# One VectorE addition moved forward in a quantised GLU kernel: the next pair's first sum ahead of two additions from the third bank

## The chip, the cores and the metric

The kernel runs on one core of one Trainium2 chip. The metric is the device time of one execution in microseconds. Before the change the median of three runs is 730.92 us (730.78 to 731.84).

A core has five engines with instruction queues of their own, each of which works strictly in order: TensorE (PE in the profile; its weight loads are PEld), VectorE (DVE), ScalarE (ACT), GpSimd (POOL) and SyncE (SP, which here only issues transfers). They wait for each other through semaphores, and so does every transfer.

## The reference

The input is `x` of 4 batches x 1024 tokens x 512 features, a condition `cond` of 4 x 128, and three weights: `norm_w`, `up_w` (4096 x 512) and `down_w` (512 x 2048). What is computed, with the quantisers written out:

```python
scale = cond @ norm_w.T + 1.0
h = x * (scale[:, None, :] * rsqrt(mean(x * x, -1) + 1e-6))
val, gate = split(h @ up_w.T, 2, axis=-1)            # 2048 features each
h = val * gelu(gate)                                  # exact gelu
s = 127.0 / clip(max(abs(h), -1), 1e-5)               # one scale for each token
hq = clip(round(h * s), -128, 127) / s
t = 1.0 / clip(mean(abs(down_w)), 1e-5)
wq = clip(round(down_w * t), -1, 1) / t               # -1, 0 or 1, times a constant
y = hq @ wq.T + x
```

So each token's hidden values become whole numbers up to 127, and the down weights become -1, 0 and 1; the down product is exact in whole numbers.

## The kernel before

**Batches and slots.** A batch is 1024 tokens in two halves of 512 (`h` = 0, 1). The up-projection of a batch is cut into 16 slots (`j` = 0 to 15); slot `j` makes 128 value features and 128 gate features for the whole batch. Batch 0 is done by plain matrix products. Batches 1 to 3 use a scheme of Winograd's kind: a block product of 2 x 2 by 2 x 2 is made with seven products in place of eight, and sums of blocks stand for the eighth. Function `slot` writes out the order of a slot: products 0, 4 and 1 of this slot, product 3 of the slot before, product 5 of this slot, product 2 of the slot before, product 6 of this slot, with the activations and additions between (all matrix products of `product` have line L580; the banks are called A, B and E).

**Down pairs.** While batch `b` is in its up slots 10 to 13 (`DOWN`), for `b` = 1 and 2, the down product of batch `b`-1 is made there: one pair (class `Pair`) in each of those four slots, number `a` = 0 to 3. A pair handles 128 tokens of each half, with the same kind of scheme: its operands are blocks of quantised values (`part(h, u)`, half of tokens and half of hidden features) and sums of them. `sum1` (L827) is `part(1,0) + part(1,1)`, 128 x 1024 in bf16, and is put into a piece of the big buffer H that the next slot will fill only later. `sums` (L834 to L836) makes the other three from it. A pair has three PSUM banks, k1, k2 and k3. Its methods, in order:

- `first`: eight matrix products of `sum1`'s result into one half of k3, then eight of `part(0,0)` into its other half (L848); ScalarE copies that half into k1 (L858).
- `third`: products into k1; ScalarE copies half of k1 to k2 (L866); then two additions on VectorE take k3's first half, times a factor for each token, onto the rows of `x` in `xr`, one for each half of tokens (`onto`, L889, 128 x 256 each).
- `fourth`: products into k1 and k2, a copy on ScalarE (L875), and an addition of 128 x 512 from k1 (L889).
- `fifth`: products into k2 and an addition of 128 x 512 from k2 (L889); then the two rows go out (L884).

The rows `xr` are loaded by SP at the head of the slot (L792, `down_load`).

**What sets the order.** The order is written out by hand: the program's order of calls is each engine's order (`manual_schedule`), and semaphores are placed by the data. `slot` calls three hooks `mid[0]`, `mid[1]`, `mid[2]`: after product 5, after product 2 with its addition (L688, `E + t2`), and after product 6 with its addition (L694, `A + v`). In a slot with a pair, `early` calls `first` and `sums` before the up products of the slot, so the first matrix product of a slot reads what `sum1` wrote in the slot before. Between the slot's own work, two lists of smaller steps (`Filler`) put the maxima and the quantising on VectorE and ScalarE by written-out costs.

**The next batch's tokens.** In the same slots the next batch is prepared (`Tokens`): load (L506), squares on ScalarE (L514), scaling on ScalarE (L526) and on GpSimd (L527, two instructions of 128 x 512), sums on GpSimd (L535 to L538), splitting (L559, L563) and a transposing transfer (L566). Some of that lies in pieces of H: token group 0's split values are in the H pieces of slots 12 and 13, and are read by the transposing transfer that is queued at the end of slot 10. `sum1` for the pair of slot 12, made in slot 11, writes the H piece of slot 12, and so waits for that transfer.

Of the kernel before, what the change touches and what calls it, by code (L numbers as in the profile page):

```python
# [50 lines left out]
def glu_quant_kernel(  # L51
# [68 lines left out]
    def t_view(b):  # L120
        v = R[:, b % 2].bitcast(F16)[:, : NA * C_ALL * 2 * HALF]
        return v.rearrange("p (a c l k t) -> p a c l k t", a=NA, c=C_ALL, l=2, k=2)
# [16 lines left out]
    def s_tile(g):  # L139


        if g >= NJ:
            return SXY[:, (g + 1) % 2]
        return S_more if g % 3 == 2 else SXY[:, g % 3]

    def h_slots(g, n=1):
        s = g % NSLOT
        return H[:, s : s + n]
# [10 lines left out]
    def po_bank(name, shape=None):  # L159
        return bank("po", 3, shape, name)  # L160
# [250 lines left out]
    def s_load_x(g):  # L411
        s_load(g, Y_TO, C_ALL)
        s_load(g, 0, Y_FROM, g % NJ >= ROWS)

    def s_load_y(g):
        if g % NJ < ROWS:
            s_load(g, Y_FROM, Y_TO)
        else:
            s_load(g, Y_FROM + 1, Y_TO)
            s_load(g, Y_FROM, Y_FROM + 1, True)  # L420
# [50 lines left out]
    def w_block(name):  # L471
        k, y = W_AT[name]
        return wd8[:, :, k, :, :, y]
# [3 lines left out]
    def d_sums(ns):  # L477
        for n, c in [(n, c) for n in ns for c in range(2)]:
            o, m, l = (w_block(name) for name in D_SUMS[n])
            DVE.tensor_tensor(o[:, c], m[:, c], l[:, c], ALU.subtract, saturate=False)  # L480
# [240 lines left out]
    def get_ready():  # L721

        POOL.partition_all_reduce(ready, ready, P, bass_isa.ReduceOp.max)
# [22 lines left out]
    def token_turn(b, am, h0=0, h1=2):  # L746

        c = slice(h0 * TOK, h1 * TOK)
        SP.dma_start(out=am_dram[b : b + 1, c], in_=am[0:1, c])

    def token_undo(b, dq, h0=0, h1=2):

        n = slice(h0 * NA, h1 * NA)
        v = am_dram[b : b + 1, h0 * TOK : h1 * TOK].rearrange("o (n p) -> p (o n)", p=P)
        SP.dma_start(out=dq[:, n], in_=v)

        def bring():
            DVE.reciprocal(dq[:, n], dq[:, n])
            DVE.tensor_scalar(dq[:, n], dq[:, n], wmean, None, ALU.mult)

        return bring
# [28 lines left out]
    def down_load(b, h, a):  # L790
        xr = wpool.tile([P, D], F32, name=f"xr_{b}_{h}_{a}", tag="xr")
        SP.dma_start(out=xr, in_=xf[rows_of(b, h, a), :])  # L792
        return xr
# [410 lines left out]
    class Filler:  # L1204
# [8 lines left out]
        def run(self, now, budget):  # L1213

            n = 0
            while n < len(self.items):
                slot, cost, f, due = self.items[n]
                assert due is None or now <= due, (now, due)
                if slot > now or (cost > budget and due != now):
                    n += 1  # L1220
                    if slot <= now:
                        break
                    continue
                del self.items[n]
                budget -= cost
                f(now)
            return budget
# [33 lines left out]
    def old_places(a):  # L1261

        if a == 0:
            v = wpool.tile([P, 2, D], F32, name="sq_0", tag="xn", bufs=1)
            u = wpool.tile([P, 4, HALF], F32, name="sr_0", tag="xt", bufs=1)
            return v[:, 0], v[:, 1], u.rearrange("p n d -> p (n d)")[:, :D]
        if a == 1:
            v = wpool.tile([P, C_ALL, 2, HALF], F16, name="sq_1", tag="nx", bufs=1)
            v = v.rearrange("p c l d -> p (c l d)").bitcast(F32)
            return [v[:, n * D : (n + 1) * D] for n in range(3)]  # L1270
        v = h_slots(B * NJ, 2).rearrange("p s h t -> p (s h) t")
        return [v[:, n] for n in range(3)]

    state = {}
    for b in range(1, B):
# [3 lines left out]
        dq = state[b - 1] = sm.tile([P, 2 * NA], F32, name=f"dq_{b}", tag="dq")  # L1279
# [41 lines left out]
        for j in range(NJ):  # L1321
            g = b * NJ + j
            down = b + 1 < B and j in DOWN
            if down:
                pair, a = pairs[j], DOWN[j]
                xrs = [down_load(b - 1, h, a) for h in range(2)]
            early_sums, late_sums = D_SUM_AT.get((b, j), ((), ()))
            left = SLOT_US + PAIR_US * down - OWN_US + 0.4
            more = D_SUM_US * len(late_sums) + 0.7 * (j + 1 == min(DOWN) and b + 1 < B)
            left -= D_SUM_US * len(early_sums) + more  # L1330
            mine = {p: [sum(c[e] for _, c in steps.get((j, p), ())) for e in range(2)] for p in "xyz"}
            left -= sum(mine[p][0] for p in "xyz")
            act_left = {"x": 2.7, "y": 2.2 if down else 1.1, "z": 0}

            def run(p):
                nonlocal left
                for f, _ in steps.get((j, p), ()):
                    f()
                if p == "x":
                    cap = min(left, 3.9 - mine["x"][0] - (0 if down else mine["y"][0] + more))  # L1340
                    left -= cap - dve.run((j, p), cap)
                elif p == "z":
                    left = dve.run((j, p), left)
                if p != "z":
                    act.run((j, p), act_left[p] - mine[p][1])

            def early():
                if down:
                    pair.first([po_bank(f"po_{b}_{a}_{n}") for n in range(3)])
                    pair.sums(None, h_slots(g)[:, 0, 1])  # L1350
                d_sums(early_sums)

            def next_pair():
                if b + 1 < B and j + 1 in DOWN:
                    pairs[j + 1] = Pair(b - 1, DOWN[j + 1])
                    pairs[j + 1].sum1(h_slots(g + 1)[:, 0, 0])

            def more_sums():
                next_pair()
                d_sums(late_sums)  # L1360

            mid = [nothing] * 3
            if j + 1 == min(DOWN):
                mid[0] = more_sums
            if down:
                mid = [lambda: (pair.third(xrs, dq), d_sums(late_sums)), lambda: (pair.fourth(), next_pair()), lambda: (loads(), pair.fifth())]

            def loads():
                if NJ + 2 <= g + 2 < B * NJ:
                    s_load_x(g + 2)  # L1370
                if NJ + 2 <= g + 1 < B * NJ:
                    s_load_y(g + 1)


            def late():
                if b == 1 and j + 1 == min(DOWN):

                    banks = [po_bank(f"po_set_{n}") for n in range(3)]
                    for bank in banks[:2]:
                        PE.matmul(  # L1380
                            bank.rearrange("p (a t) -> p a t", t=P),
                            s_tile(g + 1)[:, 0, 0, :P], t_view(b)[:, :, 0, 0, 0, :],
                            start=True, stop=True,
                        )

            if b + 1 == B and j in DOWN and DOWN[j] < 3:
                pairs[DOWN[j]] = Pair(b - 1, DOWN[j])
                places = old_places(DOWN[j])
                pairs[DOWN[j]].sum1(places[0])
                pairs[DOWN[j]].sums(*places[1:])  # L1390
            if j == 4:
                token_turn(b - 1, am)
            if j == 5:
                bring_dq = token_undo(b - 1, dq)
            if j == 6:
                bring_dq()
            if j == NJ - 1:
                get_ready()
            elif b == 1 and j == 0:
                get_ready()  # L1400
            slot(g, lambda: run("x"), lambda: run("y"), lambda: run("z"), early, mid, late)
            if not down:
                loads()
# [5 lines left out]
    dq = sm.tile([P, 2 * NA], F32, name="dq_end", tag="dq")  # L1409
# [22 lines left out]
    def old_first(a):  # L1432
        old[a].first(old_banks(a))
# [27 lines left out]
    mid = (nothing, lambda: old_first(2), nothing)  # L1461
# [105 lines left out]
```

## Time and profile before

| quantity | value |
|---|---|
| median of three runs | 730.92 us (730.78, 730.92, 731.84) |
| the profiled execution: its own time | 731.92 us |
| the profiled execution: span of the trace | 730.1 us |
| TensorE busy, of the span | 719.6 us (99%) |
| VectorE busy | 580.9 us (80%) |
| ScalarE busy | 398.5 us (55%) |
| GpSimd busy | 195.9 us (27%) |
| granted TensorE clock | 1.00 |
| slots 10, 11, 12 of batch 1, from first matrix product to first matrix product | 15.17, 16.12, 15.19 us |
| the same of batch 2 | 15.18, 16.11, 15.19 us |

The profiled execution took 731.92 us by its own clock, 1.8 us more than the span from first to last instruction, and 1.00 us more than the median. In the lists of instructions by time, a row gives the start, the length, the engine, the line of the kernel and the operation with its tiles; a bracket at the end gives the idle time of the engine just before and what ended it. A row with "x8" is eight instructions in a row. The length of a group of matrix products overlaps the next group's start, since they are pipelined: eight products of 128 x 256 take 0.87 us from start to the next group's start, though the row says 1.04. "PE po L848 <- DVE H L827: 1.5, 2, 0.8" means that L848 on TensorE waited for L827 on VectorE, 1.5 us in total, 2 times, 0.8 us at most.

### The profile page before, as it was taken

How to read it: one execution, taken by the hardware profiler on the slowest of the kernel's cores; microseconds unless marked ns; L12 is line 12 of the kernel's file. 1: busy time of each engine (PE TensorE's matmuls, PEld its weight loads, DVE VectorE, ACT ScalarE, POOL GpSimd, SP SyncE). 2: the span in 40 equal slices, each digit the busy share in tenths (PEclk: the TensorE clock that was granted, in tenths of full speed). 3: DMA queues.
4: the chain of work that ended last, by engine and by line, in shares of the span. 5: the costliest groups of instructions: out<-in, count | busy, mean ns of one | idle time of the engine just before them, and what ended most of it. 6: DMA issues, size and time to landing. Idle time of an engine off the chain costs nothing.

```text
span 730.1 us, 10143 instructions
## 1 busy us (share of the span) xinstructions
PE 719.6 (99%) x3662; PEld 359.0 (49%) x3662; DVE 580.9 (80%) x819; ACT 398.5 (55%) x629; POOL 195.9 (27%) x207
## 2 busy tenths in 40 slices
PE   7999999999999999999999999999999999999998
PEld 3544444444444446555444445656444444445844
DVE  6877879886698899787689887687678888755897
ACT  5868875872336674544335676543433665333274
POOL 1379887776100033440010030361020000000100
PEclk9999999999999999999999999999999999999999
DMA  6759999998344654876735646855934555442253
GB/s 228 259 154 312 284 275 259 236 218 230 116 102 101 131 141 131 200 165 166 185 101 103 130 101 173 199 145 156 233 92 101 94 113 102 102 102 93 93 183 115
DMA packets 203982, 117.30 MB, mean 161 GB/s; under 512 B 165382, under 2 KB 174487, under 8 KB 203932
## 3 DMA queue, kind: packets, MB, share of 16 engines
q1 hardware_dynamic: 203642, 116.33, 62.7%
q8 instruction: 28, 0.46, 0.3%
q10 hardware_dynamic: 290, 0.33, 0.1%
q14 instruction: 22, 0.18, 0.1%
HBM read 54.22 MB, written 23.09 MB: 106 GB/s over the span
## 4 chain that ended last, share of the span: by engine, by line
PE 85%; DVE 6%; POOL 3%; DMA 3%; ACT 1%; issue 1%; SPq 1%; POOLq 0%; DVEq 0%; ACTq 0%
PE A L580 33%; PE E L580 17%; PE po L848 8%; PE B L580 8%; PE pg L595 6%; PE pv L595 6%; PE po_end L800 4%; DVE gm L714 1%; DMA s_dram<-R 1%; PE po L800 1%; DMA H<-in_x_dram 1%; POOL H L372 1%; DMA SXY<-H 1%; DVE R L716 1%; ACT H L313 1%
## 5 line engine op out<-in xcount | busy, mean ns | idle before, releaser
L580 PEld LDWEIGHTS <-SXY 128*128 128x128 f16 x2016 | 197.3, 98 | 232.3 <-issue 0.6
L580 PE MATMUL A<-R,SXY 128*128 128x512 f16 x1152 | 266.3, 379 | 0.0
L580 PE MATMUL E<-R,SXY 128*128 128x512 f16 x576 | 140.0, 379 | 0.1
L678 DVE SCALAR_TENSOR_TENSOR H<-A,sg,t 128x512 f32<-128x512 f32 x48 | 36.0, 750 | 69.1 <-PE A L580 69.0
L772 DVE TENSOR_TENSOR H<-H,am 128x1024 f32<-128x1024 f32 x64 | 76.2, 1216 | 0.0
L730 POOL PARTITION_ALL_REDUCE am<-R x8 | 14.4, 1794 | 229.7 <-DVE R L716 229.7
L595 PEld LDWEIGHTS <-SXY 128*128 128x128 f16 x486 | 47.5, 98 | 57.8 <-DMA SXY<-H 0.8
L691 ACT ACTIVATE t<-t,sg 128x512 f32<-128x512 f32 x48 | 34.6, 721 | 66.7 <-DVE t L688 66.5
L580 PE MATMUL B<-R,SXY 128*128 128x512 f16 x288 | 70.0, 379 | 0.0
L714 DVE TENSOR_REDUCE gm<-H 128x512 f32<-128x1024 f32 x56 | 69.0, 1233 | 1.0
L595 PE MATMUL pg<-R,SXY 128*128 128x512 f16 x252 | 57.8, 379 | 0.3 <-DMA SXY<-H 0.3
L595 PE MATMUL pv<-R,SXY 128*128 128x512 f16 x234 | 54.4, 379 | 0.2 <-DVE H L623 0.2
L675 ACT ACTIVATE t<-B,sg 128x512 f32<-128x512 f32 x48 | 33.0, 687 | 36.5 <-PE B L580 36.5
L484 POOL TENSOR_SCALAR ssq<-ssq 128x2 f32<-128x2 f32 x12 | 4.1, 340 | 173.0 <-ACT xt L514 122.2
L658 ACT COPY t<-A 128x512 f32<-128x512 f32 x48 | 28.0, 583 | 39.5 <-PE A L580 39.2
L848 PE MATMUL po<-wd,R 128*128 128x256 fp8e4 x384 | 48.5, 273 | 0.0
L780 ACT ACTIVATE H<-H 128x1024 f32<-128x1024 f32 x38 | 39.9, 1050 | 14.1 <-DVE H L772 14.0
L670 ACT COPY v<-E 128x512 f32<-128x512 f32 x48 | 28.1, 586 | 31.2 <-PE E L580 27.7
L848 PEld LDWEIGHTS <-R 128*128 128x128 bf16 (+1 forms) x416 | 40.7, 98 | 8.5
L697 DVE SCALAR_TENSOR_TENSOR H<-v,sg,t 128x512 f32<-128x512 f32 x48 | 36.8, 768 | 7.9 <-ACT t L691 7.9
L716 DVE TENSOR_TENSOR R<-R,gm 128x512 f32<-128x512 f32 x56 | 40.9, 730 | 1.3
L784 ACT ACTIVATE R<-H 128x1024 bf16<-128x1024 f32 x38 | 40.1, 1055 | 0.8
(208 smaller groups left out, 976.4 us busy)
## 6 DMA issues: line engine op xcount, KB each, us to landing
SXY<-s_dram SPq DMA_DIRECT2D x57, 256.0 KB, 3.1
s_dram<-SXY SPq DMA_DIRECT2D x18, 384.0 KB, 3.1
H<-in_L_cond_up_w_dram SPq DMA_DIRECT2D x13, 512.0 KB, 5.1
SXY<-s_dram SPq DMA_DIRECT2D x39, 128.0 KB, 3.1
xr<-in_x_dram SPq DMA_DIRECT2D x19, 256.0 KB, 3.0
out_dram<-xr SPq DMA_DIRECT2D x19, 256.0 KB, 2.5
H<-in_x_dram SPq DMA_DIRECT2D x8, 512.0 KB, 8.4
R<-in_L_cond_down_w_dram SPq DMA_DIRECT2D x8, 512.0 KB, 6.4
```

The source lines that it names most:

```text
L580: PE.matmul(o, s[:, w, k, :], tv[:, :, c, l, k, :], start=start and n == 0, stop=stop and n == len(TERMS) - 1, skip_group_check=True,)
L595: PE.matmul(ps, a[k // 2][:, w, k % 2, :], XP[:, l, k, h * TOK : (h + 1) * TOK], start=n == 0, stop=n == len(terms) - 1,)
L678: DVE.scalar_tensor_tensor(h_half(g - 1, 0), prev["A"], gain(g - 1, 0), prev["t1"], ALU.mult, ALU.mult)
L691: ACT.activation(prev["t2"], prev["t2"], AF.Gelu, scale=gain(g - 1, 1))
L697: DVE.scalar_tensor_tensor(h_half(g - 1, 1), prev["v"], gain(g - 1, 0), prev["t2"], ALU.mult, ALU.mult)
L714: DVE.tensor_reduce(gm[0], v, AX.X, ALU.max, apply_absolute_value=True)
L716: return [largest, lambda: DVE.tensor_tensor(m, m, gm[0], ALU.max)]
L772: DVE.tensor_tensor(v, v, r.to_broadcast([P, 2, TOK]), ALU.mult)
L780: ACT.activation(v, v, AF.Copy, bias=MAGIC)
L784: ACT.activation(q, by_tile(v), AF.Copy, bias=-MAGIC)
L800: PE.matmul(po.rearrange("p (y c o) -> p y c o", c=2, o=P), q[:, a, h, j], wd8[:, :, j // n, j % n, :, y0:y1].rearrange("p c o y -> p y c o"),
L848: PE.matmul(po, w[:, j], m, start=start and j == 0, stop=stop and j == n - 1, skip_group_check=True,)
```

## The change

In a slot with a pair, the making of the next slot's `sum1` (inside `next_pair`) stood in `mid[1]`, behind `fourth`. It now stands in `mid[0]`, ahead of `third`. On VectorE the order of the instructions of a slot was: the two additions from k3 (L889), `E + t2` (L688), the addition from k1 (L889), `sum1` (L827), `A + v` (L694). It is now: `sum1` (L827), the two additions from k3, L688, the addition from k1, L694.

```diff
             if down:
-                mid = [lambda: (pair.third(xrs, dq), d_sums(late_sums)), lambda: (pair.fourth(), next_pair()), lambda: (loads(), pair.fifth())]
+                mid = [
+                    lambda: (next_pair(), pair.third(xrs, dq), d_sums(late_sums)),
+                    pair.fourth,
+                    lambda: (loads(), pair.fifth()),
+                ]
```

This touches slots 10, 11 and 12 of batches 1 and 2, six instructions in all. The pair of slot 10 gets its `sum1` in slot 9 from `more_sums`, and slot 13 has no next pair; both are as before, as is batch 3. The order on TensorE, ScalarE, GpSimd and SP is the same, and so is every operand's size. The wait of slot 11's `sum1` for the transposing transfer goes with it to its new place.

## The prediction

> **What bounds the kernel now.** I read the busy times first, then TensorE's waits, then the instructions by time around the two waits that concern the change, engine by engine.
>
> The page's first part:
>
> ```profile
> PE 719.6 (99%) x3662; PEld 359.0 (49%) x3662; DVE 580.9 (80%) x819; ACT 398.5 (55%) x629; POOL 195.9 (27%) x207
> ```
>
> TensorE has work for all but about 10 us of a 730.1 us span, at a granted clock of 1.00. So a VectorE instruction matters only where TensorE waits for it. The list of TensorE's waits from 100 us to the end has two lines:
>
> ```profile
> PE po L848 <- DVE H L827: 1.5, 2, 0.8
> PE pv L595 <- DVE H L623: 0.2, 1, 0.2
> ```
>
> The first is the moved instruction: L827 is `sum1`, L848 a pair's matrix products. It holds TensorE twice. TensorE's instructions by time show where (the last group of slot 11 and the first of slot 12 in batch 1, then the latter in batch 2):
>
> ```profile
> 305.12 1.04 PE L848 MATMUL po<-wd,R 128*128 128x256 fp8e4 x8
> 306.93 1.05 PE L848 MATMUL po<-wd,H 128*128 128x256 fp8e4 x8 [0.78 <-DVE H L827]
> ...
> 477.57 1.05 PE L848 MATMUL po<-wd,H 128*128 128x256 fp8e4 x8 [0.77 <-DVE H L827]
> ```
>
> Seen here is a distance of 1.81 us from the group at 305.12 to the next one, where groups of this form follow each other after 0.87 us elsewhere (321.25 to 322.12). Without the wait the group would start at 305.12 + 0.87 = 305.99 us, and in batch 2 (the group before starts at 475.76) at 476.63. The true loss is 0.94 us each, a little over the bracket's 0.78, since the bracket counts from the modelled end of the last product. The slots' lengths agree: slot 11 takes 16.12 and 16.11 us, its neighbours 15.17 to 15.19.
>
> VectorE in slot 11, batch 1 and then batch 2:
>
> ```profile
> 300.60 1.24 DVE L714 TENSOR_REDUCE gm<-H 128x512 f32<-128x1024 f32 x1
> 302.79 0.48 DVE L889 SCALAR_TENSOR_TENSOR xr<-po,dq,xr 128x256 f32<-128x256 f32 x1 [0.96 <-DMA xr<-in_x_dram]
> 304.17 0.49 DVE L889 SCALAR_TENSOR_TENSOR xr<-po,dq,xr 128x256 f32<-128x256 f32 x1 [0.89 <-DMA xr<-in_x_dram]
> ...
> 305.82 1.05 DVE L827 TENSOR_TENSOR H<-R 128x1024 bf16<-128x1024 bf16 x1
> ...
> 474.38 0.48 DVE L889 SCALAR_TENSOR_TENSOR xr<-po,dq,xr 128x256 f32<-128x256 f32 x1 [0.20 <-DMA xr<-in_x_dram]
> ...
> 476.03 1.48 DVE L827 TENSOR_TENSOR H<-R 128x1024 bf16<-128x1024 bf16 x1
> ```
>
> VectorE stands idle in front of the two additions from k3, because the rows of `x` have not landed (L792 is issued at 299.85, behind a long transposing transfer on SP), and `sum1`, which needs nothing of those rows, is queued behind them. GpSimd adds to it:
>
> ```profile
> 303.82 2.51 POOL L527 TENSOR_TENSOR xn<-xn,sc 128x512 f32<-128x512 f32 x2 [4.14 <-ACT xn L526]
> ...
> 474.47 2.50 POOL L527 TENSOR_TENSOR xn<-xn,sc 128x512 f32<-128x512 f32 x2 [4.14 <-ACT xn L526]
> ```
>
> GpSimd's two instructions end at 306.33 and 476.97, and `sum1` ends at 306.87 and 477.51: 0.54 us later both times, however early it began (305.82, 476.03). The four other `sum1` that the change moves also end 0.54 us behind a pair of L527 (289.39 and 289.93, 321.02 and 321.56, 460.02 and 460.56, 491.32 and 491.87), while the one at 272.38, with GpSimd idle, takes 0.68. So beside L527 this instruction ends when L527 lets it. GpSimd is released by ScalarE, which follows TensorE, so both batches lose the same, though the rows of `x` landed differently.
>
> The transfer that slot 11's `sum1` must wait for, and its time from issue to landing in that stretch (batch 1, batch 2):
>
> ```profile
> 294.83 4.93 SPq L566 DMA_TRANSPOSE R<-H  x1
> ...
> 466.00 4.63 SPq L566 DMA_TRANSPOSE R<-H  x1
> ```
>
> ```profile
> R<-H SPq DMA_TRANSPOSE x1, 6.7
> ...
> R<-H SPq DMA_TRANSPOSE x1, 6.5
> ```
>
> It lands at 294.83 + 6.7 = 301.5 and at 466.00 + 6.5 = 472.5 us.
>
> **The change, slot 11.** In batch 1 VectorE is free for the moved `sum1` from 300.60 + 1.24 = 301.84 us, 0.3 us after the transfer landed. GpSimd does nothing from 299.68 to 303.82, so I take 0.68 us from the undisturbed row: it ends at 302.52, before the first addition can start (302.79). With the slowest row, 1.48 us, it ends at 303.3; the second addition waits till 304.17 all the same. In batch 2 its last instruction before (L714, 471.24) ends at 472.47 and the transfer lands at 472.5; `sum1` ends between 473.2 and 474.0, TensorE wants it at 476.63. In both, `sum1` is done at least 2.6 us before TensorE asks. So the wait goes, if nothing stands close behind it. Next in line is the bank: the same matrix products write k3, which the second addition from k3 lets go at 304.17 + 0.49 = 304.66 and at 474.86, 1.33 and 1.77 us before the products' new starts. Their weights and the other operand were ready a slot before. So each slot 11 loses its whole excess: 16.12 - 15.18 = 0.94 and 16.11 - 15.18 = 0.93 us. Ends for this term: nothing at all, if something unseen stands at the same place, and 1.87, since TensorE loses no more there.
>
> **The change, slots 10 and 12.** Here `sum1` was in time already (done 0.88 and 0.56 us ahead of TensorE in batch 1, 0.90 and 0.89 in batch 2), so nothing is to be gained, and the question is what now comes later: the two additions from k3 (which free k3 for the next slot's first product), L688 (which ScalarE's gelu L691 waits for), and the addition from k1. `A + v` (L694) and all that follows has the same work in front of it as before.
>
> Batch 2 hides it simply. VectorE has 0.73 us idle in front of L688 in both slots, and the new starts (456.15, and 487.45 less the shift) lie more than a microsecond before L527 (457.52, 488.82), so `sum1` takes 0.68 and L688 starts within 0.1 us of its old time: cost 0.
>
> In batch 1, slot 10, `sum1` would start at 286.78, beside L527 (286.88 to 289.39). If it comes first it takes 0.68; if it waits for both instructions of L527 it ends at 289.93, the two additions take 0.87 more, and k3 is free at 290.7, with TensorE asking at 290.81. Slot 12 is the densest stretch: `sum1` would start near 318, and L527 sits there, 0.94 us earlier than before, from 317.3 to 320.1. At worst `sum1` ends at 320.1 + 0.54 = 320.6, k3 is free at 321.5, and TensorE asks at 322.12 - 0.94 = 321.18: a cost of 0.3 us. If it gets in after the first instruction of L527 (half of 2.83 us: 318.7), k3 is free at 320.1 and the cost is 0. I take 0, which all but the full hold give, and keep +0.3 as the end. L691 may start up to 1.1 us later in slot 12; what it feeds, L697, writes values that are not read on TensorE's way before the next batch, so this costs nothing. If L527 is held by `sum1` instead, its sums (done at 293.06 in slot 10) are read by L559 at 301.25: 8 us of cover.
>
> The Trainium skill's page "SBUF — State Buffer", section "SBUF: two separate sides", says that VectorE and GpSimd share a pair of ports as an exclusive lock, held for a whole instruction, also by a VectorE instruction with two SBUF inputs against a GpSimd one that reads SBUF. That fits the six ends 0.54 us behind L527, and it speaks against the change in slots 10 and 12, where `sum1` now meets L527 at its start. By the page the lock is given up between the two instructions, which would put that cost at 0 and the sum at -1.87; by the worst reading of the rows the sum is -1.57.
>
> **Queues.** SP, GpSimd, ScalarE and TensorE keep their orders. SP's L884 behind `fifth` waits for an addition that in slot 11 comes no later than before (L694 moves from 306.80 to about 305.8, the addition after it waits for TensorE until 306.2). The wait for the transfer is now in front of two additions, L688 and the addition from k1; but the rows of `x` are issued on SP behind that same transfer, so those additions could not start before it anyway.
>
> **The sum.** -0.94 - 0.93 + 0 = -1.87 us. TensorE has no other wait from slot 12 to the end, and the steps that feed it there (loads of weights, transposed tokens, scales) are released by TensorE or by VectorE's work, which moves forward with it. The last transposing transfer of batch 2's tokens is the closest I found: issued at 346.30, landing some 6.4 us later at 352.7, first read near 355.4, so 2.7 us of cover against a shift of 0.94. The profiled execution's own 731.92 us would become 730.05; it stands 1.00 us above the median, so the median of 730.92 becomes 729.05, or 0.26% less.
>
> **The rivals.** (1) The wait changes its owner: TensorE waits for k3 instead, as rows of `x` that land later would hold the additions. For it: the rows land late (304.17, 474.38). Against it stand 1.33 and 1.77 us of room. With half of one place's gain and the worst of slot 12, it comes to 730.92 - 1.87 + 0.47 + 0.3 = 729.8. The case that the timed executions lose less there than the profiled one belongs here too.
>
> (2) Slower: slot 11's `sum1` is held by the transposing transfer, with the additions behind it. It lands at 301.5 and 472.5; from landing on, `sum1` and two additions need 0.68 + 0.87 us, so TensorE waits only for a landing after 304.4 and 475.1, and the kernel gets slower than before only from 305.4 and 476.0 on, 3.5 us late. The twelve transfers of this line landed 6.0 to 7.5 us after issue, so about 1 us of scatter is seen. At 4.5 us late in both the price is 2 x 1.0 us: 732.9.
>
> (3) The change does nothing: TensorE waits in truth for something else at 306.93. Against it: the weight load of the same products, which reads only `sum1`'s result, starts at 306.93 as well, 0.06 us after `sum1` ends, and in batch 2 also. Time: 730.9.
>
> **How the numbers follow.** About 0.2% (1.46 us) is what a measurement of this kernel can tell from no change, and the predicted gain is only 0.41 us beyond it, with runs that spread over 1.06 us. The forecast has 0.72, of which I give 0.05 to scatter that hides it; rival 1 has 0.18, of which 0.03 still reaches 0.2%; rival 3 has 0.06, rival 2 0.04. Faster: 0.72 - 0.05 + 0.03 = 0.70. Slower: 0.04. Same: the rest, 0.26. The range goes from 728.4 (the whole gain and 0.65 us of scatter, somewhat over half of the runs' spread) to 730.5 (rival 1 and 0.7 us of scatter); rivals 2 and 3 are left out.
>
> **What would show it.** Right: TensorE's list of waits has no L827, the slots 11 take 15.2 us, `sum1` of slot 11 starts at about 301.8 and 471.6 (the second 0.94 earlier than now reckoned) and takes near 0.7, and the additions start still at the rows' landing. The step for slots 10 and 12 is wrong if a slot after them starts late with TensorE waiting for L889. The prediction as a whole is wrong if a new wait of about 0.9 us stands at slot 12's start with another releaser, or if TensorE's shift of 0.94 is lost again before slot 0 of the next batch.

## The result and the profile after

The changed kernel takes 730.02 us (median of 22 runs, 728.83 to 731.95), the kernel before, timed beside it, 731.61 us (median of 22 runs, 729.67 to 734.85). The ratio is 0.9978, with a 95% interval of 0.9968 to 0.9988: 0.22% faster, 1.6 us between the medians. The runs spread with the granted clock: the fifteen of the changed kernel with a mean of 0.999 or 1.000 have a median of 729.62 us, the seven with 0.997 or 0.998 one of 731.39. The profiled execution took 730.04 us, with a span of 728.3 us against 730.1 before.

The list of TensorE's waits from 100 us to the end has lost its first line:

```profile
PE pv L595 <- DVE H L623: 0.2, 1, 0.2
```

TensorE's instructions by time, the last group of slot 11 and the first of slot 12, in batch 1 and in batch 2:

```profile
305.14 1.04 PE L848 MATMUL po<-wd,R 128*128 128x256 fp8e4 x8
306.01 1.04 PE L848 MATMUL po<-wd,H 128*128 128x256 fp8e4 x8
...
474.83 1.04 PE L848 MATMUL po<-wd,R 128*128 128x256 fp8e4 x8
475.71 1.04 PE L848 MATMUL po<-wd,H 128*128 128x256 fp8e4 x8
```

The groups now follow each other after 0.87 and 0.88 us, where 1.81 us lay between them before. VectorE in slot 11 of batch 1 (start, length, instruction, idle time in front of it):

```profile
300.62 1.24 DVE L714 TENSOR_REDUCE gm<-H 128x512 f32<-128x1024 f32 x1
301.77 0.69 DVE L827 TENSOR_TENSOR H<-R 128x1024 bf16<-128x1024 bf16 x1
302.67 0.48 DVE L889 SCALAR_TENSOR_TENSOR xr<-po,dq,xr 128x256 f32<-128x256 f32 x1 [0.22 <-issue]
303.74 0.48 DVE L889 SCALAR_TENSOR_TENSOR xr<-po,dq,xr 128x256 f32<-128x256 f32 x1 [0.58 <-DMA xr<-in_x_dram]
```

`sum1` fills time in which VectorE stood idle. The second addition still starts when its row lands; for the first the bracket names no releaser ("issue"), so that it waits for its row is not shown here. All six slots with a moved `sum1` take 15.18 us from first product to first product; slot 11 took 16.12 and 16.11. By batch 2's slot 13 TensorE is 1.88 us ahead of before (a group of the pair's products there stands at 502.15 against 504.03), and it keeps that to the end: 730.1 - 728.3 = 1.8 us.

One more place is worth a look, for what follows. In slot 12 of batch 1, `sum1` took 1.76 us. VectorE's instructions and GpSimd's L527 there, before the change and then after it:

```profile
317.97 0.68 DVE L716 TENSOR_TENSOR R<-R,gm 128x512 f32<-128x512 f32 x1
...
320.61 0.95 DVE L827 TENSOR_TENSOR H<-R 128x1024 bf16<-128x1024 bf16 x1
...
318.19 2.83 POOL L527 TENSOR_TENSOR H<-H,sc 128x512 f32<-128x512 f32 x2 [2.03 <-ACT H L526]
```

```profile
316.87 0.68 DVE L716 TENSOR_TENSOR R<-R,gm 128x512 f32<-128x512 f32 x1
317.47 1.76 DVE L827 TENSOR_TENSOR H<-R 128x1024 bf16<-128x1024 bf16 x1
319.15 0.86 DVE L889 SCALAR_TENSOR_TENSOR xr<-po,dq,xr 128x256 f32<-128x256 f32 x2
...
317.25 3.11 POOL L527 TENSOR_TENSOR H<-H,sc 128x512 f32<-128x512 f32 x2 [2.19 <-ACT H L526]
```

After the change the two additions let k3 go at 320.01 and TensorE asks at 321.19, so nothing waits in this execution.

### The profile page after: what moved, and what is told of

Its sections match the earlier page's. It is cut to its first block, busy times and chain, and to the rows that moved or that the text cites. A ratio compares the mean times of both kernels' runs of the same rounds, so it can differ in the third digit from the quotient of the medians.

```text
span 728.3 us, 10143 instructions
## 1 busy us (share of the span) xinstructions
PE 719.1 (99%) x3662; PEld 359.2 (49%) x3662; DVE 578.8 (79%) x819; ACT 398.7 (55%) x629; POOL 194.9 (27%) x207
## 4 chain that ended last, share of the span: by engine, by line
PE 84%; DVE 5%; POOL 3%; DMA 3%; ACT 2%; issue 1%; SPq 1%; POOLq 0%; ACTq 0%; DVEq 0%
PE A L580 33%; PE E L580 17%; PE po L848 8%; PE B L580 8%; PE pg L595 6%; PE pv L595 5%; PE po_end L800 4%; DVE gm L714 1%; PE po L800 1%; DMA H<-in_x_dram 1%; ACT H L313 1%; POOL R L387 1%; DMA SXY<-H 1%; DMA xa<-in_x_dram 1%; DVE R L716 1%
## 5 line engine op out<-in xcount | busy, mean ns | idle before, releaser
L595 PEld LDWEIGHTS <-SXY 128*128 128x128 f16 x486 | 47.5, 98 | 57.9 <-DMA SXY<-H 0.8
L595 PE MATMUL pg<-R,SXY 128*128 128x512 f16 x252 | 57.8, 379 | 0.3 <-DMA SXY<-H 0.3
L595 PE MATMUL pv<-R,SXY 128*128 128x512 f16 x234 | 54.4, 379 | 0.2 <-DVE H L623 0.2
L697 DVE SCALAR_TENSOR_TENSOR H<-v,sg,t 128x512 f32<-128x512 f32 x48 | 37.6, 783 | 7.9 <-ACT t L691 7.9
L694 DVE TENSOR_TENSOR v<-A,v 128x512 f32<-128x512 f32 x48 | 32.8, 684 | 11.8 <-PE A L580 10.6
L716 DVE TENSOR_TENSOR R<-R,gm 128x512 f32<-128x512 f32 x56 | 40.9, 731 | 1.3
```

Source lines behind the costliest of these rows:

```text
L595: PE.matmul(ps, a[k // 2][:, w, k % 2, :], XP[:, l, k, h * TOK : (h + 1) * TOK], start=n == 0, stop=n == len(terms) - 1,)
L697: DVE.scalar_tensor_tensor(h_half(g - 1, 1), prev["v"], gain(g - 1, 0), prev["t2"], ALU.mult, ALU.mult)
L716: return [largest, lambda: DVE.tensor_tensor(m, m, gm[0], ALU.max)]
```

## The experiments

The theory to test: the gain is slot 11's wait alone. The wait before was made of two things, rows of `x` that landed late in front of `sum1`, and GpSimd's L527, which held `sum1` when it came to run. The rivals: slots 10 and 12 have a share; the rows alone, or GpSimd alone, made the wait; the transfer that `sum1` waits for can turn the gain into a loss. In all of them the lengths of slots are taken from first product to first product, and "excess" is what a slot has over 15.18 us. The ratio beside two medians is an estimate of its own, with its 95% interval in brackets; it can differ from the quotient of the medians by 0.1%.

**Slot 11 alone (e1)**

```diff
+front = j == 11
-    lambda: (next_pair(), pair.third(xrs, dq), d_sums(late_sums)),
-    pair.fourth,
+    lambda: (next_pair() if front else None, pair.third(xrs, dq), d_sums(late_sums)),
+    lambda: (pair.fourth(), None if front else next_pair()),
```

> Only slot 11's first sum stands in front; slots 10 and 12 keep the order of before. Theory (all of the gain is slot 11's wait): TensorE has no wait for the first sum in the down slots, slot 11 takes 15.18 us in batches 1 and 2, and the time is 1.87 us below the kernel before, a ratio of 0.9974, the same as the full change. Rival (the order in slots 10 and 12 does something too, for better or worse): the time differs from the full change's by more than 0.3 us, and slots 10 to 12 differ from it in the trace.

Measured: 730.14 us against 731.46, ratio 0.9976 (0.9965 to 0.9987), as for the full change. Slot 11 has no excess in either batch. But the profile has a new wait, in a slot that was quiet before. TensorE, VectorE and GpSimd of that execution around slot 12 of batch 1:

```profile
321.99 1.05 PE L848 MATMUL po<-wd,H 128*128 128x256 fp8e4 x8 [1.19 <-DVE H L827]
...
317.00 1.76 DVE L716 TENSOR_TENSOR R<-R,gm 128x512 f32<-128x512 f32 x1
...
320.73 1.21 DVE L827 TENSOR_TENSOR H<-R 128x1024 bf16<-128x1024 bf16 x1
...
316.69 3.20 POOL L527 TENSOR_TENSOR H<-H,sc 128x512 f32<-128x512 f32 x2 [1.78 <-ACT H L526]
```

Slot 12 takes 16.53 us. L527 began 0.3 us ahead of L716 here, L716 took 1.76 us in place of 0.68, and `sum1`, at its old place behind it, came too late for a TensorE that asks 0.94 us sooner. So slot 12 isn't idle ground. The timed runs do not show this loss as clearly as the profile, whose own time (730.87 us) is the slowest of its eight.

**Slots 10 and 12 alone (e2)**, the condition of e1 turned round (`j != 11`).

> Only the first sums of slots 10 and 12 stand in front; slot 11 keeps the order of before. Theory: nothing is gained or lost, ratio 1.000; slot 11 still takes 16.1 us and TensorE still waits 0.8 us twice for the first sum; in slot 12 of batch 1 the first sum is held by GpSimd's scaling and takes 1 us or more, with TensorE not waiting. Rival (slots 10 and 12 share the gain or cost something): the ratio lies at 0.999 or lower, or a slot 11 or 13 starts late.

Measured: 731.74 against 731.46, ratio 0.9998 (0.9986 to 1.001): no change that can be told from none. Slot 11 of batch 1 has its excess of 0.94. In batch 2 it has none, which was not expected. There `sum1` started at 476.45, while L527 ran from 475.46 to 478.42, and it took 0.84 us: it got in before GpSimd's second instruction. In the kernel before it started at 476.03 with L527 from 474.47, inside the second one. So the old wait depends on where in L527 `sum1` falls, and a slot 11 in the old order does not lose its 0.94 us in every execution.

**Behind the two additions from k3 (e3)**

```diff
-    lambda: (next_pair(), pair.third(xrs, dq), d_sums(late_sums)),
+    lambda: (pair.third(xrs, dq), next_pair(), d_sums(late_sums)),
```

> In all three slots the first sum stands behind the two additions from k3 and in front of E + t2: later than in the change, earlier than before, and still behind the late rows of x. It starts near 304.2 to 304.6 us in slot 11 of batch 1, inside GpSimd's first scaling instruction (303.8 to 305.1). Theory (the port is given up between GpSimd's two instructions, and the first sum ends 0.54 us behind the one that it met): it ends at 305.6, 0.4 us before TensorE asks at 306.0, so the whole 1.87 us is won, with the rows as late as before: it was not needed to pass the late rows, only to begin before GpSimd's second instruction. Rival A (the late rows are the cause): some of the wait is left, 0.3 us or more in each slot 11. Rival B (GpSimd's pair holds it as one): it ends at 306.9 as before and the time is that of before.

Measured: 730.21 against 731.46, ratio 0.9981 (0.9971 to 0.9992). VectorE, GpSimd and TensorE in slot 11 of batch 1:

```profile
304.47 0.48 DVE L889 SCALAR_TENSOR_TENSOR xr<-po,dq,xr 128x256 f32<-128x256 f32 x1 [0.49 <-DMA xr<-in_x_dram]
304.87 1.06 DVE L827 TENSOR_TENSOR H<-R 128x1024 bf16<-128x1024 bf16 x1
...
304.11 2.95 POOL L527 TENSOR_TENSOR xn<-xn,sc 128x512 f32<-128x512 f32 x2 [4.14 <-ACT xn L526]
...
306.28 1.04 PE L848 MATMUL po<-wd,H 128*128 128x256 fp8e4 x8
```

`sum1` ends at 305.93, in the middle of the pair of L527, and the pair takes 2.95 us in place of 2.50: VectorE came between the two instructions. TensorE does not wait in slot 11 of either batch. Both rivals fall in this run: the rows were as late as ever, and the pair did not hold as one. This agrees with what the page "SBUF — State Buffer" of the Trainium skill says in its section "SBUF: two separate sides": whichever of the two instructions starts first holds the shared pair of ports "for the whole instruction". Slot 12 of batch 1 has an excess of 0.32 here, with L527 (317.52) ahead of L716 (318.29).

**The order of before, with the rows of `x` early and the transfer late (e4)**; **the changed order with the same (e5)**

```diff
 plan, token group 0:
-    ((6, "z"), (7, "x"), (7, "y"), (9, "y"), (10, "x"), (10, "z"))
+    ((6, "z"), (7, "x"), (7, "y"), (9, "y"), (10, "x"), (11, "x"))
```

> The order of before on VectorE, but token group 0's transposing transfer is queued on SP behind slot 11's rows of x in place of ahead of them, so the rows come early (near 300 us) and the transfer lands late, by an estimate at 304.9 us (rows issued at 297.1, transfer 1.1 later, 6.7 to land). VectorE reaches the first sum by about 304.2 and waits for the transfer. Theory (late rows plus GpSimd's second scaling instruction made the wait): if the transfer lands before 305.1 the first sum ends at 305.6 and TensorE does not wait, 1.87 us faster than before; if it lands later, the first sum ends at 306.9 and nothing is gained. Rival (only VectorE's order counts): the wait of 0.94 us stays in both batches whatever lands when.

> The changed order on VectorE, with the transposing transfer behind the rows of x: this makes the slower rival happen. The first sum now waits in front of the two additions until the transfer lands, near 304.9 us by the same estimate. Theory: it ends at 305.6, the two additions end at 306.4, and TensorE waits 0.4 to 0.5 us in each slot 11, for k3 (L889), not for the first sum: about 1 us slower than the change, 0.9 us faster than before. If the transfer lands after 305.1, the first sum ends at 306.9, the additions at 307.7, TensorE waits 1.7 us each time, and the kernel is 1.5 us slower than before. Rival (the wait for the transfer is harmless at either place): as fast as the change.

Measured for e4: 732.21 against 731.66, ratio 0.9998 (0.9983 to 1.0014). In its profile slot 11 has no excess in either batch: `sum1` waited for the transfer until 304.33, met L527 (303.70) in its first instruction and ended at 305.52, and TensorE asked at 305.87. So VectorE's order is not the only way to take this wait away, and the rival falls. Yet slot 12 of batch 1 took 16.30 us, 1.12 of excess, again with L527 (317.11) ahead of L716 (317.17). That leaves 0.75 us of gain in the profile. The 1.87 us of the theory did not come in the timed runs: six of the twelve had a mean granted clock of 0.995 to 0.998 (median 732.87 us), and the six with 0.999 or 1.000 have a median of 730.74, against 731.16 for twenty such runs of the kernel before. What each of them lost in slot 12 is not shown.

Measured for e5: 731.59 against 731.66, ratio 0.9997 (0.9985 to 1.0009). VectorE, GpSimd and TensorE of batch 1:

```profile
302.79 1.69 DVE L827 TENSOR_TENSOR H<-R 128x1024 bf16<-128x1024 bf16 x1 [2.12 <-DMA R<-H]
304.40 0.86 DVE L889 SCALAR_TENSOR_TENSOR xr<-po,dq,xr 128x256 f32<-128x256 f32 x2
...
317.07 1.76 DVE L716 TENSOR_TENSOR R<-R,gm 128x512 f32<-128x512 f32 x1
...
302.65 2.95 POOL L527 TENSOR_TENSOR xn<-xn,sc 128x512 f32<-128x512 f32 x2 [4.14 <-ACT xn L526]
...
316.56 3.40 POOL L527 TENSOR_TENSOR H<-H,sc 128x512 f32<-128x512 f32 x2 [1.58 <-ACT H L526]
...
305.32 1.05 PE L848 MATMUL po<-wd,H 128*128 128x256 fp8e4 x8 [0.33 <-DVE xr L889]
321.36 1.05 PE L848 MATMUL po<-wd,H 128*128 128x256 fp8e4 x8 [0.69 <-DVE xr L889]
```

The first wait is the slower rival: `sum1` stands still for the transfer, the additions stand behind it, and TensorE waits for k3. It costs 0.49 and 0.48 us in the two slots 11, as expected, though the transfer landed earlier than estimated (`sum1` was let go at 302.8, in an execution that reached slot 11 about 1.2 us sooner). L527 has a part in it: `sum1` met its first instruction and took 1.69 us; with 0.68 us k3 would have been free near 304.3, by an estimate, ahead of TensorE, which asked at 304.83. The second wait, 0.86 us of excess in slot 12 of batch 1, was not expected, and makes the sum 1.83 us, about what the kernel before loses. It has the same root: from `sum1` at 302.79 to L716 at 317.07 VectorE has no gap of more than 0.1 us, so what slot 11 lost in time brought L716 behind L527. So the gain hangs on where the transfer is queued.

**The order of before, with GpSimd's scaling later (e6)**

```diff
 plan, token group 2:
-    ((10, "y"), (11, "x"), (11, "y"), (13, "x"), (13, "y"), (13, "z"))
+    ((10, "y"), (11, "x"), (11, "z"), (13, "x"), (13, "y"), (13, "z"))
```

> The order of before on VectorE, but the scaling of token group 2 (ScalarE's L526 and with it GpSimd's L527) stands one place later in slot 11, behind ScalarE's gelu of that slot, so GpSimd is idle while the first sum runs. Theory (the wait was made of lateness behind the rows of x, and of GpSimd's hold on top): the first sum starts where it did (305.8 and 476.0) and takes 0.68 us, ends at 306.5 and 476.7, and TensorE's excess per slot 11 falls from 0.94 to about 0.57 in batch 1 and 0.14 in batch 2; 1.2 us faster than before. Rival A (the late rows alone): the wait stays 0.94. Rival B (GpSimd alone): the wait is gone, 1.87 us faster.

Measured: 732.14 against 731.66, ratio 1.0002 (0.999 to 1.0014); the 1.2 us of the theory did not come. Slot 11 is as expected in kind: `sum1` takes 0.68 us in both batches, and the excess falls to 0.51 and 0.40 us (0.57 and 0.14 expected; in batch 2 the second row was there 2.0 us before TensorE asked, 2.25 in the first profile of before). With GpSimd away about half of the wait stays; with the rows early and GpSimd in place (e4) none stayed. So both causes are real. But L527 and its sums now lie in VectorE's way at the head of slot 12 (L716 at 308.38 takes 1.75 us), whose excess in batch 1 is 1.98 us, and more than the gain is lost there.

**Slots 11 and 12 (e7), and second profiles (e8, e9, e10)**

The profiles of e1 and e3 to e6 all show trouble in slot 12 of batch 1, which the kernel before does not have. The theory was reworked: TensorE's 0.94 us bring L527 forward, since it follows TensorE (in all 14 profiles L527 of slot 12 in batch 1 starts 11.24 to 11.26 us after the slot's first product), and L716 on VectorE comes only just ahead of it or just behind. e7 is e1 with `front = j > 10`; e8, e9 and e10 are e1, the kernel before and the changed kernel once more.

> First sums of slots 11 and 12 in front, slot 10's where it was before. Theory, reworked after the runs so far (slot 11's move wins the wait; slot 12's move is needed in batch 1 to keep the gain, since TensorE then asks 0.94 us sooner; slot 10's move is worth nothing): TensorE has no wait in the down slots and the ratio is that of the full change, 0.9975 to 0.998. Rival (slot 10 matters too): TensorE waits at slot 11's start, or slot 10 is longer than 15.2 us.

> A second profile of the kernel with slot 11 alone moved. Theory (where VectorE's L716 meets GpSimd's L527 in slot 12 of batch 1 is settled anew in each execution): if L716 starts before L527 it takes 0.68 us and TensorE's wait at slot 13 is 0 to 0.4 us; if after, it takes 1.76 and the wait is again 1.2. Rival (the wait at slot 13 is there in every execution): 1.2 us whichever comes first.

> A second profile of the kernel before. Theory: TensorE waits for the first sum in slot 11 where the first sum starts after GpSimd's second L527 instruction, 0.8 us by the bracket, and does not where it starts earlier, as in batch 2 of the run with slots 10 and 12 alone; so one, two or no waits. Rival (the wait is the same in each execution): two waits of 0.8 us.

> A second profile of the changed kernel. Theory: no wait of TensorE for L827 or L889 from 100 us on, slots 10 to 12 at 15.2 us in both batches, first sum of slot 12 of batch 1 between 0.7 and 1.8 us. Rival (the first profile was a lucky one): a wait of 0.3 us or more in one of the slots.

e7: 730.48 against 732.2, ratio 0.9981 (0.9965 to 0.9998); slot 10 takes 15.18 us in both batches, so its `sum1` is worth nothing. The theory's other half fails: slot 12 of batch 1 has 0.66 us of excess, waiting for L889, with L527 (316.99) ahead of L716 (317.30).

e8: no wait at all, with L716 ahead of L527:

```profile
318.88 0.69 DVE L716 TENSOR_TENSOR R<-R,gm 128x512 f32<-128x512 f32 x1
...
321.53 0.95 DVE L827 TENSOR_TENSOR H<-R 128x1024 bf16<-128x1024 bf16 x1
...
319.26 2.67 POOL L527 TENSOR_TENSOR H<-H,sc 128x512 f32<-128x512 f32 x2 [2.19 <-ACT H L526]
```

So e1's wait is there in one execution and not in another, and goes with that order. (e8's own time, 732.04 us, is still longer than e1's 730.87: its slot 10 of batch 1 began at 277.67 us in place of 275.10, ahead of all that is at issue here; its granted clock in the first 50 us was 0.97, in e1 1.00.)

e9: the two old waits of 0.77 and 0.78 us, as in the first profile of the kernel before; `sum1` started in L527's second instruction both times.

e10: the changed kernel has a wait after all. TensorE, VectorE and GpSimd:

```profile
321.84 1.05 PE L848 MATMUL po<-wd,H 128*128 128x256 fp8e4 x8 [0.48 <-DVE xr L889]
...
304.25 0.48 DVE L889 SCALAR_TENSOR_TENSOR xr<-po,dq,xr 128x256 f32<-128x256 f32 x1 [0.69 <-DMA xr<-in_x_dram]
...
307.16 1.23 DVE L697 SCALAR_TENSOR_TENSOR H<-v,sg,t 128x512 f32<-128x512 f32 x1
...
307.12 0.72 POOL L536 TENSOR_TENSOR xt<-xn 128x256 f32<-128x256 f32 x1
...
317.56 1.76 DVE L716 TENSOR_TENSOR R<-R,gm 128x512 f32<-128x512 f32 x1
319.24 1.75 DVE L827 TENSOR_TENSOR H<-R 128x1024 bf16<-128x1024 bf16 x1
320.92 0.86 DVE L889 SCALAR_TENSOR_TENSOR xr<-po,dq,xr 128x256 f32<-128x256 f32 x2
...
317.25 3.19 POOL L527 TENSOR_TENSOR H<-H,sc 128x512 f32<-128x512 f32 x2 [1.78 <-ACT H L526]
```

L527 starts at the same 317.25 as in the first profile of the changed kernel, but L716 at 317.56 in place of 316.87. Now L716 waits for L527's first instruction and `sum1` for its second, and the additions behind them let k3 go at 321.78; slot 12 takes 15.83 us. Where L716 lost its 0.69 us can be read back to slot 11. There the second row of `x` let its addition go at 304.25 in place of 303.74, so L697 (value times gelu, VectorE's last work for that slot) began at 307.16 in place of 306.93. GpSimd's sum L536 begins at 307.12 in both profiles, so L697 is ahead of it in the first and behind it here, and takes 1.23 us in place of 0.77; from there to L716 VectorE has no gap of more than 0.1 us. In e12, the third profile of the change, and in e8, L697 is ahead of L536 as well; in e1 and e7 it is behind. So the order in slot 12 is settled a slot earlier, and the late rows of slot 11 have a part in it. The rival of a lucky first profile is half right.

**Slot 12's sum further forward (e11), and the change timed beside it (e12)**

```diff
-    lambda: (next_pair(), pair.third(xrs, dq), d_sums(late_sums)),
+    lambda: (next_pair() if j < 12 else None, pair.third(xrs, dq), d_sums(late_sums)),
...
-slot(g, lambda: run("x"), ...)
+slot(g, lambda: (next_pair() if down and j == 12 else None, run("x")), ...)
```

> The change, and slot 12's first sum moved further forward, ahead of the splitting of token group 1 (L563) and of L716, near 314.8 us, about 2 us before GpSimd's L527 of that slot. Theory (what the change still loses is slot 12 of batch 1, where L527 may come ahead of L716 and then of the first sum): the first sum takes 0.7 us, L716 may still take 1.76, the additions from k3 end near 320.2, 1 us before TensorE asks at 321.2; no wait in any slot, whichever comes first, and a time 0.3 us below the change on average. Rival (the later work in slot 12 eats it): a wait for L889 of 0.3 us or more at slot 13's start remains.

> The changed kernel once more, timed beside the version with slot 12's first sum further forward. Theory: ratio to before 0.9975 to 0.9985; in the profile either no wait, if L716 starts before L527 in slot 12 of batch 1, or a wait of TensorE of about 0.5 us for L889 at slot 13's start, if after. Rival: a wait that does not go with that order.

Measured: e11 730.08 against 731.42, ratio 0.9976 (0.9966 to 0.9986); e12 729.8, ratio 0.9981 (0.997 to 0.9992). The two cannot be told apart by time, so the 0.3 us expected of e11 is not shown. The profile of e11 had the bad order, and shows what it was made for (VectorE, GpSimd, TensorE, batch 1):

```profile
317.03 0.68 DVE L827 TENSOR_TENSOR H<-R 128x1024 bf16<-128x1024 bf16 x1
...
319.71 1.76 DVE L716 TENSOR_TENSOR R<-R,gm 128x512 f32<-128x512 f32 x1
321.39 0.86 DVE L889 SCALAR_TENSOR_TENSOR xr<-po,dq,xr 128x256 f32<-128x256 f32 x2
...
319.44 3.16 POOL L527 TENSOR_TENSOR H<-H,sc 128x512 f32<-128x512 f32 x2 [2.15 <-ACT H L526]
...
323.38 1.04 PE L848 MATMUL po<-wd,H 128*128 128x256 fp8e4 x8
```

L527 is ahead of L716, which takes 1.76 us, and still k3 is free at 322.25, 1.1 us before TensorE asks; slot 12 takes 15.18 us (from 308.20). In the profile of e12, L716 (315.57) came ahead of L527 (315.88), and there was no wait. Over all 14 profiles, L716 ahead of L527 goes with no excess in slot 12 of batch 1 (the kernel before twice, the change twice, e2, e8), and L527 ahead with some (e1, e3 to e7, e10), except in e11, which was built to stand it.

## Why the prediction was right or wrong, step by step

**What bounds the kernel: right.** From 100 us on, TensorE's two waits for L827 are its only waits in both profiles of the kernel before, but for one of 0.2 us in the first (L595).

**Slot 11: right, in place and size.** `sum1` was predicted at about 301.8 and 471.6 us with 0.7 us each; it ran at 301.77 (0.69) and 471.47 (0.68). The second additions started at their rows' landing, the slots took 15.18 us where 15.2 was forecast. The profiled execution's 731.92 was to become 730.05; it became 730.04. That they agree to 0.01 us is luck: both executions began slot 10 of batch 1 at 275.6 us, where the other profiles lie between 274.28 and 277.84. e2 shows that without slot 11 no gain can be seen.

**The reading of L527: right, and sharper than put.** `sum1` ends 0.54 us behind the instruction of L527 that it met; e3 showed that this is one of the two instructions and not the pair, which the prediction's rows had left open. e4 and e6 showed that the late rows and L527 both made the old wait, and e3 that `sum1` need not pass the rows if it gets in before the second instruction.

**Slots 10 and 12: the step that was mis-sized.** Slot 10 is worth nothing and costs nothing, as put (e7): in batch 1 `sum1` begins 0.08 us ahead of L527 (286.81 and 286.89) and takes 0.68 us. For slot 12 of batch 1 the prediction took 0, with +0.3 as its end. The changed kernel loses 0 in two profiles and 0.65 us in the third, where TensorE waits for L889 behind slot 12: the sign that the prediction itself gave for this step being wrong. The end was worked out with `sum1` held by the whole of L527; missed was that L716, just in front of it on VectorE, is held as well, one instruction each. And "nothing is to be gained" there holds only against the old TensorE: once it is 0.94 us ahead, `sum1` at its old place is late in slot 12, by 1.35 us in e1's profile and not at all in e8's. The same mechanism costs less in the change, since `sum1` is already ahead.

**The sum.** -1.87 us was forecast, and the medians of 22 runs differ by 1.59. The interval of the ratio (2.3 to 0.9 us) holds -1.87 too, so the rest need not mean anything. Two things are known that would make it: the changed kernel's loss of 0.65 us in part of the executions, and a kernel before that does not lose 0.94 us in each slot 11 every time (e2's batch 2, in the old order there, lost none). How often either comes was not counted. Among runs with a granted clock of 0.999 or 1.000, the medians differ by 1.88 us in e12 (8 runs against 19) and by 1.3 to 1.4 us in its variants e1, e3, e7 and e11. The median itself, 730.02 us, lies 0.97 above the 729.05 of the forecast; 0.69 of that is the start, since the kernel before has 731.61 over 22 runs and had 730.92 over three.

**The rivals.** In one profile of three the wait did change its owner, as rival 1 said, to L889 and k3, but a slot later: in e10 a later row in slot 11 had a part in bringing L716 behind L527 in slot 12. The slower rival's mechanism exists: e5 brought it about and lost the gain; in the three profiles of the change as made it stays out, as put. Its bounds were mis-sized, since they gave `sum1` 0.68 us: in e5, beside L527, it took 1.69 and 1.54, and TensorE lost 0.49 and 0.48 us with `sum1` let go 13.1 and 13.3 us after the slot's start, where the prediction had 13.6 as harmless. Its price was mis-added, too: by the prediction's own bounds, 4.5 us late gives 0.6 and 1.0 us, not 2 x 1.0, so 732.5 us. And of the twelve transfers that are said to land after 6.0 to 7.5 us, the trace has eight landings. That the change does nothing is refuted by e1 and e2, and by TensorE's list of waits.

## What to carry to other kernels

When an instruction on a busy engine is waited for, look at what stands idle in front of it in its queue: here the engine had time to spare while it waited for something that the instruction did not need. After a wait is taken from the engine that sets the pace, look at every engine that follows it one place further on; all of it moves forward, and two instructions that just missed each other may now meet. A loss that is there in one profile and not in the next is found by taking the profile again, by finding the order of two starts that goes with it, and by reading back what set that order.

## What the runs showed of the hardware that was not expected

A VectorE instruction with both inputs in SBUF that meets GpSimd's product there is held until that GpSimd instruction is over: `sum1` and L716 then end 0.54 to 0.55 us after it, in each of the 53 cases in the 14 profiles in which one of them began inside an instruction of L527. They take up to 1.77 us, where both need 0.68 us alone. It comes in between two GpSimd instructions that follow each other directly, and the pair of those is then longer, 2.95 us for 2.50. L688 and the 128 x 256 additions of L889, which read one operand from PSUM, took 0.67 to 0.69 and 0.47 to 0.49 us beside L527 in all profiles. Which engine comes first is settled by tenths of a microsecond: 316.87 or 317.56 us for L716 against 317.25 for L527, in two executions of one program, made the difference between no wait and 0.65 us of TensorE's time.
